# A two-layer graph network on one core: the order of the random walks, the projections' stationary, and how layer 1's targets reach the partitions

## The chip, the cores and the metric

The kernel runs on one core of a Trainium2 chip, in float32. The metric is the device time of one execution in microseconds (us). Engines are named as the profile names them: PE (TensorE matmul) with PEld (its weight load), DVE (VectorE), ACT (ScalarE), POOL (GpSimd), SP (SyncE, which here only issues DMAs).

## The reference

x has N = 2708 nodes of D = 256 features, adj is N x N. Two layers, each with a residual and a layer norm:

```
# layer 0
R = (adj + I) / rowsum
for n in (0, 1):
    A  = top_p(softmax((Xa W1^T W2^T)(Xa W3^T)^T), 0.9), rows renormalized
    Xf = R Xf;  Xa = A Xa                 # both start from x
    Z += Xf U1[n]^T + Xa U2[n]^T
x = layernorm(x + (layernorm(x + Z) * g + b))
# layer 1, 4 heads of 64
Wh = x W;  s_i = Wh a_src;  s_j = Wh a_dst
att = softmax_j(leaky_relu(s_i + s_j, 0.2) where adj != 0 or i == j)
x = layernorm(x + att Wh)
```

The part with R (the "walks") is R x U1[0]^T + R R x U1[1]^T. The part with A is the "attention".

## The kernel before, in words

The nodes are cut into NT = 22 row tiles (16 of 128 rows, 6 of 110). A block of the transposed adjacency is the stationary of a walk matmul, and 22 of them give one tile of a walk; there are two walks, so 2 x 22 x 22 = 968 walk matmuls (`walks()`, L845). The blocks come from memory by half tiles on SP's queue (`load`, through `by_tile`, L94), three buffers deep (`adjp`). A walk accumulates in the one PSUM bank of pool `ps_wk`.

**Layer 0, start.** `load_x` brings x into `xe` (its last column is 1, so the first walk also gives the row sums). Six groups of tiles are turned (PE transposes, L1045) and projected (L1056): a stationary `wq` = W1^T W2^T written twice side by side gives q on both halves of the partitions, and a second stationary `wk_sb` (W3^T twice) gives k on both. Both halves are needed because `scores` (L620) works on the two halves of the columns at once, with k of columns 0 to 1353 on partitions 0 to 63 and of the others on 64 to 127.

**The order written by hand.** After this, PE, ACT, DVE and POOL follow an order made by Python generators. SP and everything outside that block are ordered by the framework's planner. `slot(spend, begin)` advances the running searches (`going`) by one piece, may start the search of a later tile, advances the open epilogues (`doing`), and then emits `spend` walk matmuls (it stops at the end of a tile's walk; what is left of the spend is kept for the next slot). There are 10 slots in the fill, then in `step(0)` 22 tiles of 6 slots, a stretch between the steps, `step(1)` again with 22 tiles of 6 slots, and a tail. The spends are:

```python
SPEND_FIRST, SPEND_0 = 5, (2, 2, 2, 2, 2, 1)
SPEND_BETWEEN, SPEND_1 = 6, (5, 5, 4, 5, 5, 4)
```

In `step`, `weigh` transposes the attention weights `e` of the tile by groups (L202), ACT copies them (`eT`, L208) one group ahead, and PE multiplies (L217). A search is: scores on PE, exponentials on ACT (L624), in step 1 four passes of ACT over the row (L645), then candidates and sorting on DVE (L710 to L797). It starts three tiles ahead.

**Epilogues.** `after_walk0(t)`: DVE adds the tile's own row to the walk result (L858), PE turns it (`turn`, L603), and `terms1` (L890) multiplies it by both U1 matrices: one part goes, scaled and summed, to `c1` in memory, the other becomes `yw`, the input of walk 1. `after_attention0(t)`: turns the attention result, projects a pair of tiles for step 1 (`project`, L591), and `terms2` (L910) multiplies by both U2 matrices. `finish(t)`: ACT scales walk 1's result (L924), POOL adds `c1`, `c2` and the attention result held in `held`, then two layer norms, and `sources` computes layer 1's values and scores.

**Layer 1.** Targets are taken in three spans of 8, 8 and 6 tiles. `targets` puts exp(0.8 s_i) of a span on all partitions: for each tile and head a transpose with a broadcast stationary (L174) and an exponential on ACT (L179). Span 0's are made by `first_targets` during the last tile of step 1. Then for each of 22 source tiles: load the mask block (L1164), ACT makes it 0/1 (L1165, L1170), DVE forms four heads of weights (L1225), PE multiplies them (L1233, L1240). `settle` finishes a span.

Of the kernel before, what the change touches and what calls it, by code (L numbers as in the profile page):

```python
# [16 lines left out]
P = 128  # L17
# [19 lines left out]
SPEND_FIRST, SPEND_0 = 5, (2, 2, 2, 2, 2, 1)  # L37
SPEND_BETWEEN, SPEND_1 = 6, (5, 5, 4, 5, 5, 4)
HELD = 8
# [6 lines left out]
def kernel(  # L46
# [71 lines left out]
    def load_x():  # L118
        step = 4
        for t0 in range(0, NT, step):  # L120
            by_tile(xe[:, t0:, 0:D], x, t0, min(t0 + step, NT))
# [45 lines left out]
    def targets(g, r, aux):  # L167

        i0 = off[spans[g][0]]
        for t in spans[g]:  # L170
            m = rows[t]
            tr = aux()
            for h in range(H):
                nc.tensor.transpose(  # L174
                    tr[:, h, :m], s_src[:m, t, h : h + 1].to_broadcast([m, P]),
                    ident[:m, :m],
                )
            for k in range(2):
                nc.scalar.activation(  # L179
                    r[k][:, :, off[t] - i0 : off[t + 1] - i0], tr[:, 2 * k : 2 * k + 2, :m],  # L180
                    AF.Exp, scale=1.0 - NEG_SLOPE,
                )
            yield
# [41 lines left out]
    def general_layer0():  # L225
        with ExitStack() as l0:
# [8 lines left out]
            load_x()  # L235
# [248 lines left out]
    def fast_layer0(ep, adjp):  # L484
# [22 lines left out]
        wq = w0.tile([P, DC, 2, DA], F32, name="wq")  # L507
        wk_sb = w0.tile([P, DC, 2, DA], F32, name="wk_sb")
# [4 lines left out]
        w2_sb = tmp[:DA, P : 2 * P].rearrange("p (h e) -> p h e", h=2)  # L513
        w1_sb = heldp.tile([P, D], F32, name="xa1")[:DA].rearrange("p (c d) -> p c d", c=DC)
        nc.scalar.dma_start(w1_raw, w1T.rearrange("(c p) e -> p c e", p=P))
        for h in range(2):
            nc.scalar.dma_start(w2_sb[:, h, :], w2T)
        for h in range(2):
            nc.scalar.dma_start(wk_sb[:, :, h, :], w3T.rearrange("(c p) e -> p c e", p=P))
        load_x()  # L520
# [33 lines left out]
        yw = keep.tile([P, NT, D], F32, name="yw")  # L554
# [6 lines left out]
        c2 = [dram.tile([P, D], F32, name=f"c2_{t}") for t in range(NT)]  # L561

# [8 lines left out]
        for c in range(DC):  # L571
            tr = ps_tr.tile([P, 4, P], F32, name="tr")
            nc.tensor.matmul(
                tr[:, 0, :], w1_sb[:, c, :], w2_sb.rearrange("p h e -> p (h e)"),
                start=True, stop=True,
            )
            nc.vector.tensor_copy(wq[:, c].rearrange("p h e -> p (h e)"), tr[:, 0, :])

        def keep_k(s, c0, m, src, copy):
            low = max(0, min(HN - c0, m))  # L580
            if low:
                copy(kT[s][0:DA, c0 : c0 + low], src[0:DA, :low])
            if low < m:
                copy(kT[s][DA:P, c0 + low - HN : c0 + m - HN], src[DA:P, low:m])

        def project(s, c0, w, xT, copy_q, copy_k):

            pj = ps_tr.tile([P, 4, P], F32, name="tr").rearrange("p (n a) b -> p n (a b)", n=2)
            for n, wm in enumerate((wq, wk_sb)):
                for c in range(DC):  # L590
                    nc.tensor.matmul(  # L591
                        pj[:, n, :w], wm[:, c].rearrange("p h e -> p (h e)"), xT[:, c, :w],
                        start=(c == 0), stop=(c == DC - 1),
                    )
            copy_q(qT[:, c0 : c0 + w], pj[:, 0, :w])
            keep_k(s, c0, w, pj[:, 1], copy_k)
# [216 lines left out]
        def walks():  # L813
# [16 lines left out]
            for n, (s, t, j0, j1) in enumerate(queue):  # L830
                m = rows[t]
                cur, w = (xe, D + 1) if s == 0 else (yw, D)
# [5 lines left out]
                if j0 == 0:  # L838
                    ac = ps_wk.tile([P, CHUNK], F32, name="walk")
                    if s:  # L840
                        ca, cb = (finp.tile([P, D], F32, name=k) for k in ("ca", "cb"))
                        nc.sync.dma_start(ca[:m], c1[t][:m])
                        nc.sync.dma_start(cb[:m], c2[t][:m])
                for j in range(j0, j1):
# [4 lines left out]
                    if j == NT - 1:  # L849
                        doing.append(after_walk0(t, ac) if s == 0 else finish(t, ac, ca, cb))  # L850
# [3 lines left out]
        def after_walk0(t, ac):  # L854
            m = rows[t]
            unfinished.add(t)
            xf = rowp.tile([P, D + 1], F32, name="xf")
            nc.vector.tensor_add(xf[:m], ac[:m, : D + 1], xe[:m, t, :])  # L858
            nc.vector.reciprocal(rinv[:m, t : t + 1], xf[:m, D : D + 1])
            yield  # L860
            tp = ps_tr.tile([P, 4, P], F32, name="tr")
            xT = turn(xf, m, tp, nc.scalar.copy)
            yield
            terms1(t, xT)
# [4 lines left out]
        def after_attention0(t, xa):  # L869
# [10 lines left out]
            if t % 2:  # L880
                project(1, off[t - 1], 2 * m, both, nc.scalar.copy, nc.scalar.copy)
# [3 lines left out]
        def terms1(t, xT):  # L885
# [3 lines left out]
            for c in range(DC):  # L889
                nc.tensor.matmul(  # L890
                    cy[:m], xT[:, c, :m], u_sb[:, 0, c].rearrange("p s e -> p (s e)"),
                    start=(c == 0), stop=(c == DC - 1),
                )
            r = rinv[:m, t : t + 1]
            cs = rowp.tile([P, D], F32, name="cs")
            nc.scalar.activation(cs[:m], cy[:m, 0:D], AF.Copy, scale=r)
            nc.scalar.activation(yw[:m, t, :], cy[:m, D : 2 * D], AF.Copy, scale=r)

            own = rowp.tile([P, D], F32, name="own", bufs=1)
            nc.gpsimd.tensor_scalar(own[:m], yw[:m, t, :], r, None, op0=ALU.mult)  # L900
            nc.gpsimd.tensor_add(cs[:m], cs[:m], own[:m])
# [410 lines left out]
```

## Time and profile before

| | us |
|---|---|
| median of 3 runs | 1678.13 (1677.03 to 1678.82) |
| the profiled execution, its time | 1677.58 |
| the profiled execution, its span | 1675.8 |
| granted PE clock, mean | 0.992 |
| PE busy | 1610.0 |
| DVE busy | 1217.0 |
| ACT busy | 766.8 |
| POOL busy | 423.4 |
| first scores on PE (L620) | at 40.3 |
| first attention matmul of step 0 (L217) | at 71.7 |
| first attention matmul of step 1 | at 655.0 |
| last attention result of step 1 (L1005) | at 1280.0 |
| first matmul of layer 1 (L1233) | at 1298.1 |

The span runs from the first to the last instruction; the time also has what lies around it. "Busy" is the time in which an engine had an instruction running; a busy PE is not PE at its peak. A float32 matmul shows as two records in the profile, a transpose as one. In a table by stage each column gives an engine's busy us in that stretch and, in brackets, its instructions; behind them stand the granted PE clock, the share of the DMA engines' time, and GB/s.

### The profile page before, as it was taken

The page shows a single profiled execution, that of the slowest core. Times are in us where ns is not written, and L with a number is a line of the kernel's source. Part 1 is how long each engine was busy: PE and PEld are TensorE (multiplying, and loading weights), DVE is VectorE, ACT ScalarE, POOL GpSimd, SP SyncE. Part 2 cuts the span into 40 slices and gives each one's busy share as a digit, 9 for nine tenths or more (in the row PEclk, how much of TensorE's full clock was granted, in tenths as well). Part 3 has the DMA queues.
Part 4 walks back from the last instruction along what each step waited for, and adds up shares of the span by engine and source line. Part 5 has one row for each costly group of instructions (what it writes and reads, how often), then busy time and mean ns, then how long its engine had stood idle before and what let it go on. Part 6 is the DMA issues. An engine that isn't in the chain of part 4 may idle for free.

```text
span 1675.8 us, 23985 instructions
## 1 busy us (share of the span) xinstructions
PE 1610.0 (96%) x8218; PEld 1058.0 (63%) x8218; DVE 1217.0 (73%) x3660; ACT 766.8 (46%) x1324; POOL 423.4 (25%) x893
## 2 busy tenths in 40 slices
PE   7999999999999999999999999999997999999895
PEld 4677777777777776777787878777785222322332
DVE  2954554565455019888999999998994899888886
ACT  1333333333333255656576666667555334243231
POOL 0310111111011023223244444444434020420313
PEclk9999999999999999999999999999999999999998
DMA  6211011111110142212322322323222332232231
GB/s 166 73 47 46 26 43 40 40 31 40 40 43 25 43 104 67 63 49 73 79 72 79 87 68 82 89 58 77 72 65 88 98 99 86 88 93 77 76 86 39
DMA packets 153873, 113.89 MB, mean 68 GB/s; under 512 B 39898, under 2 KB 144094, under 8 KB 153742
## 3 DMA queue, kind: packets, MB, share of 16 engines
q1 hardware_dynamic: 149278, 105.18, 23.4%
q0 software_dynamic: 2112, 5.55, 1.0%
q10 hardware_dynamic: 2352, 1.54, 0.3%
q8 instruction: 67, 1.10, 0.3%
q14 instruction: 64, 0.52, 0.1%
HBM read 101.16 MB, written 11.09 MB: 67 GB/s over the span
## 4 chain that ended last, share of the span: by engine, by line
PE 78%; DVE 9%; ACT 5%; POOL 4%; issue 3%; DMA 0%; ACTq 0%; POOLq 0%; DVEq 0%; SPq 0%
PE att L217 23%; PE walk L845 19%; PE acc L1233 12%; PE acc L1240 6%; PE lg L620 5%; PE tr L202 4%; ACT e L624 3%; PE tr L910 2%; PE tr L890 2%; PE lg L1056 1%; PE tr L591 1%; DVE cand L725 1%; ACT eT L208 1%; DVE scr L791 1%; POOL res L1192 1%
## 5 line engine op out<-in xcount | busy, mean ns | idle before, releaser
L645 ACT ACTIVATE junk<-e,minus,rth 128x2708 bf16<-128x2708 f32 (+1 forms) x88 | 232.8, 2646 | 35.7 <-POOL rth L677 34.6
L845 PE MATMUL walk<-xe,blk 128*128 128x257 f32 (+3 forms) x968 | 240.5, 382 | 0.0
L217 PE MATMUL att<-ba,eT 128*128 128x256 f32 (+3 forms) x968 | 234.1, 383 | 5.0 <-ACT eT L208 5.0
L217 PE MATMUL att<-xe,eT 128*128 128x256 f32 (+3 forms) x968 | 233.3, 381 | 4.3 <-ACT eT L208 4.3
L208 ACT COPY eT<-tr 128x512 f32<-128x512 f32 (+5 forms) x264 | 138.2, 537 | 206.3 <-PE tr L202 206.1
L1233 PE MATMUL acc<-pt,v 128*64 128x512 f32 (+3 forms) x1056 | 226.0, 550 | 4.7 <-DVE pt L1225 3.8
L845 PE MATMUL walk<-yw,blk 128*128 128x256 f32 (+3 forms) x968 | 228.1, 381 | 1.7 <-ACT xw L924 1.7
L725 DVE MAX8 cand<-e 128x8 f32<-128x170 f32 (+1 forms) x352 | 89.2, 322 | 178.8 <-ACT e L624 178.8
L845 PEld LDWEIGHTS walk<-xe,blk 128*128 128x128 f32 (+3 forms) x968 | 174.6, 186 | 54.2 <-issue 29.3
L845 PEld LDWEIGHTS walk<-yw,blk 128*128 128x128 f32 (+3 forms) x968 | 176.7, 186 | 41.5 <-issue 11.5
L1225 DVE SCALAR_TENSOR_TENSOR pt<-e,tj,blk 128x1024 f32<-128x1024 f32 (+3 forms) x176 | 185.8, 1115 | 19.8 <-issue 8.0
L217 PEld LDWEIGHTS att<-ba,eT 128*128 128x128 f32 (+3 forms) x968 | 171.4, 186 | 32.7 <-ACT eT L208 10.0
L217 PEld LDWEIGHTS att<-xe,eT 128*128 128x128 f32 (+3 forms) x968 | 170.9, 186 | 30.9 <-ACT eT L208 7.2
L624 ACT ACTIVATE e<-lg 128x1024 f32<-128x1024 f32 (+1 forms) x132 | 121.1, 921 | 132.3 <-PE lg L620 132.3
L1233 PEld LDWEIGHTS acc<-pt,v 128*64 128x64 f32 (+1 forms) x1056 | 72.1, 137 | 153.5 <-issue 112.3
L202 PE MATMUL tr<-ident,e 128*128 128x128 f32 (+3 forms) x968 | 140.8, 270 | 4.6 <-ACT xT L606 3.8
L202 PEld LDWEIGHTS tr<-ident,e 128*128 128x128 f32 (+3 forms) x968 | 115.1, 139 | 32.3 <-ACT xT L606 6.1
L1165 ACT ACTIVATE blk<-blk 128x1024 f32<-128x1024 f32 (+3 forms) x66 | 63.2, 958 | 155.3 <-DMA blk<-in_adjT_dram 136.3
L1240 PE MATMUL acc<-pt,sb 128*32 128x512 f32 (+3 forms) x1056 | 124.5, 549 | 0.0
L1225 DVE SCALAR_TENSOR_TENSOR pt<-r,tj,blk 128x1024 f32<-128x1024 f32 (+1 forms) x88 | 109.8, 1306 | 10.8 <-issue 7.0
L631 POOL TENSOR_TENSOR fact<-zp 128x1 f32<-128x1 f32 (+1 forms) x44 | 24.8, 563 | 359.0 <-ACT e L624 349.1
L725 DVE MAX8 cand<-scr 128x8 f32<-128x97 f32 (+1 forms) x616 | 101.9, 243 | 0.0
(203 smaller groups left out, 1999.6 us busy)
## 6 DMA issues: line engine op xcount, KB each, us to landing
blk<-in_adjT_dram SPq DMA_DIRECT2D x32, 704.0 KB
blk<-in_adjT_dram SPq DMA_DIRECT2D x32, 512.0 KB
blk<-in_adjT_dram SPq DMA_DIRECT2D x48, 330.0 KB
blk<-in_adjT_dram SPq DMA_DIRECT2D x32, 320.0 KB
blk<-in_adjT_dram SPq DMA_DIRECT2D x12, 605.0 KB
blk<-in_adjT_dram SPq DMA_DIRECT2D x12, 440.0 KB
blk<-in_adjT_dram SPq DMA_DIRECT2D x18, 283.6 KB
c<-cs POOLq DMA_DIRECT2D x32, 128.0 KB, 2.1
```

Source lines behind the costliest of these rows:

```text
L202: nc.tensor.transpose(tr[: rows[t], q, :m], e[:m, off[t] : off[t + 1]], ident[:m, :m])
L208: copy(eT[:k, : len(grp), :m], tr[:k, : len(grp), :m])
L217: nc.tensor.matmul(acc, eT[: rows[t], q, :m], value(t), start=(t == 0), stop=(t == NT - 1),)
L620: nc.tensor.matmul(lg[:m, h, :w], qT[part, cols], kT[s][part, c0 : c0 + w], start=True, stop=True,)
L624: nc.scalar.activation(halves[:m, :, c0 : c0 + w], lg[:m, :, :w], AF.Exp, accum_out=zp[:m, n : n + 1],)
L645: nc.scalar.activation(junk[:m], e[:m], func, scale=rth, bias=minus1[:m], accum_out=acc)
L725: nc.vector.max(cand[:, n, :], src[:m, n * size : min(N, (n + 1) * size)])
L845: nc.tensor.matmul(ac[:m, :w], blk[: rows[j], j - j0, :m], cur[: rows[j], j, 0:w], start=(j == 0), stop=(j == NT - 1),)
L1165: nc.scalar.activation(bar, bar, AF.Sign)
L1225: nc.vector.scalar_tensor_tensor(pt[:k, :gw], r[h // 2][:k, h % 2, :gw], tj[:k, j, h : h + 1], mask, op0=ALU.max, op1=ALU.mult,)
L1233: nc.tensor.matmul(acc[h // 2][c][q * FO : (q + 1) * FO, :w], v[j][:k, h - 1 + q, :], pts[h - 1 + q][:k, c0 : c0 + w], **at,)
L1240: nc.tensor.matmul(acc[2][c][h * 32 : (h + 1) * 32, :w], sb[:k, j, h : h + 1].to_broadcast([k, 32]), pts[h][:k, c0 : c0 + w], **at,)
```

## The change

It has five parts.

1. **Walks factored.** The walk part is computed as R (x U1[0]^T + R (x U1[1]^T)). `terms1` no longer follows walk 0: it works on the turned x that the projections have made anyway (kept in `x_turned`, in the space of `ba`), writes x U1[0]^T to `c1` and x U1[1]^T into `xe`. x itself now lies in `xm`, which attention step 0 reads. Walk 0 runs on `xe`; its epilogue divides by the row sum, adds `c1` and overwrites x in `xm`, on DVE and POOL alone. Walk 1 runs on `xm`. `finish` loads x again from memory.
2. **The order.** No walk matmul is emitted in the fill or in step 0; the ten slots of the fill emit `terms1` instead. The spends of the other stretches rise. `finish` has fewer empty slots.
3. **One stationary for q and k.** k and q columns stand side by side in one stationary (`wkqk`), so one matmul pair gives k on the half where it is wanted and q on the other half; a DMA on POOL's queue copies q to the half where k is. A range that crosses column 1354 is cut there.
4. **Attention results of step 1** for tiles 0 to 17 go to memory (`c3`, on POOL's queue) and come back when the tile's second walk begins (on SP's queue).
5. **Targets through memory.** `share` makes one transpose and one exponential for a whole span (32 rows: tile and head) and stores it; `spread` reads it back with four DMAs of SP, each onto all 128 partitions.

```diff
-SPEND_FIRST, SPEND_0 = 5, (2, 2, 2, 2, 2, 1)
-SPEND_BETWEEN, SPEND_1 = 6, (5, 5, 4, 5, 5, 4)
-HELD = 8
+SPEND_BETWEEN, SPEND_1 = 7, (7, 6, 7, 7, 6, 7)
+HELD, WAITING = 6, 4
...
+    def share(g, tr):
+        span, m = spans[g], rows[spans[g][0]]
+        k = len(span) * H
+        nc.tensor.transpose(
+            tr[:k, 0, :m],
+            s_src[:m, span[0] : span[-1] + 1, :].rearrange("p t h -> p (t h)"), ident[:m, :m],
+        )
+        nc.scalar.activation(line[:k, :m], tr[:k, 0, :m], AF.Exp, scale=1.0 - NEG_SLOPE)
+        nc.sync.dma_start(shared[g], line[:k, :m])
+
+    def spread(g, r):
+        lines = shared[g].rearrange("(t h) m -> h t m", h=H)
+        n = len(spans[g]) * rows[spans[g][0]]
+        for k in range(2):
+            for h in range(2):
+                nc.sync.dma_start(
+                    r[k][:, h, :n].rearrange("p (t m) -> p t m", t=len(spans[g])),
+                    lines[2 * k + h].partition_broadcast(P),
+                )
...
+        def project(s, c0, w, pj, xT, copy_q, copy_k):
+            for lo, hi, h in ((c0, min(c0 + w, HN), 0), (max(c0, HN), c0 + w, 1)):
...
                 for c in range(DC):
                     nc.tensor.matmul(
-                        pj[:, n, :w], wm[:, c].rearrange("p h e -> p (h e)"), xT[:, c, :w],
-                        start=(c == 0), stop=(c == DC - 1),
+                        pj[:, at], wkqk[:, c, h : h + 2].rearrange("p h e -> p (h e)"),
+                        xT[:, c, at], start=(c == 0), stop=(c == DC - 1),
                     )
-            copy_q(qT[:, c0 : c0 + w], pj[:, 0, :w])
-            keep_k(s, c0, w, pj[:, 1], copy_k)
+                copy_k(kT[s][here, lo - h * HN : hi - h * HN], pj[here, at])
+                copy_q(qT[there, lo:hi], pj[there, at])
+                nc.gpsimd.dma_start(qT[here, lo:hi], qT[there, lo:hi])
...
-                cur, w = (xe, D + 1) if s == 0 else (yw, D)
+                cur, w = (xe, D + 1) if s == 0 else (xm, D)
...
+                    ca = finp.tile([P, D], F32, name="ca", bufs=4)
                     if s:
-                        ca, cb = (finp.tile([P, D], F32, name=k) for k in ("ca", "cb"))
+                        cb = finp.tile([P, D], F32, name="cb")
+                        nc.sync.dma_start(ca[:m], x[off[t] : off[t + 1], :])
+                        nc.sync.dma_start(cb[:m], c2[t][:m])
+                        if t in c3:
+                            held[t] = finp.tile([P, D], F32, name="cc")
+                            nc.sync.dma_start(held[t][:m], c3[t][:m])
+                    else:
                         nc.sync.dma_start(ca[:m], c1[t][:m])
-                        nc.sync.dma_start(cb[:m], c2[t][:m])
...
         def after_walk0(t, ac, ca):
...
             nc.vector.tensor_add(xf[:m], ac[:m, : D + 1], xe[:m, t, :])
-            nc.vector.reciprocal(rinv[:m, t : t + 1], xf[:m, D : D + 1])
+            nc.vector.reciprocal(r, xf[:m, D : D + 1])
             yield
-            tp = ps_tr.tile([P, 4, P], F32, name="tr")
-            xT = turn(xf, m, tp, nc.scalar.copy)
-            yield
-            terms1(t, xT)
+            nc.gpsimd.tensor_scalar(xf[:m, :D], xf[:m, :D], r, None, op0=ALU.mult)
+            nc.gpsimd.tensor_add(xm[:m, t, :], xf[:m, :D], ca[:m])
...
         def terms1(t, xT):
...
-            nc.scalar.activation(cs[:m], cy[:m, 0:D], AF.Copy, scale=r)
-            nc.scalar.activation(yw[:m, t, :], cy[:m, D : 2 * D], AF.Copy, scale=r)
-
-            own = rowp.tile([P, D], F32, name="own", bufs=1)
-            nc.gpsimd.tensor_scalar(own[:m], yw[:m, t, :], r, None, op0=ALU.mult)
-            nc.gpsimd.tensor_add(cs[:m], cs[:m], own[:m])
-            nc.gpsimd.tensor_add(cs[:m], cs[:m], xe[:m, t, 0:D])
+            nc.scalar.copy(cs[:m], cy[:m, 0:D])
+            nc.scalar.copy(xe[:m, t, 0:D], cy[:m, D : 2 * D])
             nc.gpsimd.dma_start(c1[t][:m], cs[:m])
...
         def finish(t, ac, ca, cb):
-            nc.scalar.activation(xw, ac[:m, :D], AF.Copy, scale=rinv[:m, t : t + 1])
+            nc.vector.tensor_add(xw, ac[:m, :D], xm[:m, t, :])
             yield
+            nc.scalar.activation(xw, xw, AF.Copy, scale=rinv[:m, t : t + 1])
...
         def step(s, cur, spend):
+                if s and t == NT - 2:
+                    share(0, ps_tr.tile([P, 4, P], F32, name="tr"))
                 if s and t == NT - 1:
-                    doing.append(first_targets())
+                    ahead.extend(room(ep))
+                    spread(0, ahead)
...
-                        if s:
+                        if s and t in c3:
+                            nc.gpsimd.dma_start(c3[t][:m], xa[:m])
+                            stored.add(t)
+                        elif s:
                             held[t] = xa
...
             for n in range(10):
-                slot(SPEND_FIRST if n else 0, (0, n // 4) if n in (0, 4, 9) else None)
+                slot(0, (0, n // 4) if n in (0, 4, 9) else None)
+                for t in range(n * NT // 10, (n + 1) * NT // 10):
+                    terms1(t, x_turned[:, :, off[t] : off[t + 1]])
             layer1_weights()
-            step(0, xe, SPEND_0)
+            step(0, xm, [0] * len(groups))
...
-                    list(targets(g + 1, r_next, aux))
+                    share(g + 1, aux())
+                    spread(g + 1, r_next)
```

## The prediction

> **What bounds the kernel now.** I read the page first, then a table of busy time by stage, then the chain of waits inside one step-0 tile, then the time line of the first 30 us.
>
> The page says that TensorE (PE) is full nearly everywhere:
>
> ```profile
> span 1675.8 us, 23985 instructions
> ...
> PE 1610.0 (96%) x8218; PEld 1058.0 (63%) x8218; DVE 1217.0 (73%) x3660; ACT 766.8 (46%) x1324; POOL 423.4 (25%) x893
> ...
> PE   7999999999999999999999999999997999999895
> ...
> DVE  2954554565455019888999999998994899888886
> ```
>
> Only 66 us of the span are without PE work. DVE is half idle in slices 5 to 17 and nearly full in slices 18 to 29. The stage table (busy us of PE, PEld, DVE, ACT, POOL) puts that in numbers: fill of the pipeline, attention step 0, the stretch between, step 1, the gap before layer 1, layer 1.
>
> ```profile
> 43.00:71.00 28.00, 27.48 (x123) 19.55 (x120) 25.92 (x94) 7.56 (x17) 10.26 (x13) 1.00 0.32 82
> 71.00:588.00 517.00, 509.18 (x2440) 376.51 (x2439) 261.27 (x958) 172.00 (x387) 56.41 (x124) 1.00 0.14 39
> 588.00:654.00 66.00, 62.70 (x269) 43.99 (x268) 28.27 (x109) 36.26 (x51) 21.01 (x49) 1.00 0.38 98
> 654.00:1280.00 626.00, 614.95 (x3026) 482.42 (x3024) 562.15 (x2094) 402.00 (x659) 244.52 (x550) 1.00 0.27 70
> 1280.00:1298.00 18.00, 11.26 (x63) 8.00 (x60) 11.18 (x16) 10.68 (x46) 11.25 (x14) 0.91 0.55 166
> ```
>
> So moving walk matmuls from step 0 to step 1 moves PE time, it does not remove it. What counts is PE work deleted, and waits that appear or go where the walks served as filler. The chain through a step-0 tile shows the one place where filler already covers a wait:
>
> ```profile
> 235.80 1.08 PE lg L620 x4
> ...
> 236.91 2.12 ACT e L624 x4
> 239.03 0.48 ACT eT L208
> ...
> 239.56 2.00 PE att L217 x8
> ...
> 242.68 0.87 PE walk L845 x4
> ```
>
> At the head of a tile the first attention matmul waits for two exponentials and a copy on ACT, 3.76 us after the scores begin, whatever PE does meanwhile. Behind it the chain is PE alone. A "walk x4" piece is two matmuls (two records each): 0.435 us a walk matmul.
>
> **The change part by part.** Unit prices from that chain and its neighbours: walk matmul 0.435, `terms1` or `terms2` 1.72, `turn` about 0.4 with its wait, `project` of a tile pair 1.73, targets of one tile 0.44 (four transposes, as "tr x4").
>
> How many walk matmuls each stage holds I counted by stepping the hand-written order: slots times spend. Before: 44 in the fill, 243 in step 0, 96 between, 585 in step 1. After: 0, 0, 110, 858. Both sum to 968.
>
> *First projections.* The time line:
>
> ```profile
> 10.73 3.78 PE L1056 MATMUL lg<-e,wq 128*128 128x512 f32 x4 [0.99 <-ACT e L1051]
> ...
> 18.28 1.99 PE L1056 MATMUL lg<-e,wq 128*128 128x512 f32 x4 [0.67 <-ACT e L1051]
> 20.10 1.88 PE L1056 MATMUL lg<-e,wk_sb 128*128 128x512 f32 x4
> ```
>
> A group repeats every 5.3 us; one stationary for q and k deletes the second matmul pair: 1.7 us for each of three warm full groups, 1.46 and 0.73 for the short ones, about 2.4 for the first: 9.7 us. The copies (0.6 on ACT, 0.7 on DVE per group) fit in the 3.5 us that remain. The first row runs at half the later speed. [...] By the row, speed came at about 15 us after some 4.5 us without a break; the changed order still has 3.4 us of slow matmuls and 1.3 of transposes in a row. I take +1, and keep 0 to +10.7.
>
> The second copy of q goes through a POOL-issued SBUF transfer, whose cost for this path is not in the trace; nearest row: `c<-cs`, 2.1 us to landing, issue about 0.6. The first scores read columns copied four groups earlier, so 0 if they wait only for these, +3 if for the last copy. I take +1. Sum of the part: -7.7, scores start near 32.5 instead of 40.3.
>
> *Fill.* Out: 44 walks (19.1), one `turn` and `terms1` (2.1). In: all 22 `terms1`, 37.8 us. Net +16.6. Each has 0.75 us of ACT copies and a 0.65 us DMA issue on POOL, under 1.72 of PE; `cs` has two buffers, so its round trip (copy, issue, 2.1 landing: about 3.4) just fits two `terms1`. If it didn't, 0.3 us each, +6: upper end.
>
> *Step 0.* A tile pair lasts 48.4 us in the chain. Out: 20 of its 22 walks (8.7), the two at the heads being worth nothing because ACT's 3.76 us stands; a `turn` (0.4), a `terms1` (1.8), half a `project` (0.86). That is 11.8 a pair, 36.6 left; 11 pairs give -129. DVE falls from 11.9 us a tile to about 11.6 against 18.3, so it does not become the bound; searches start three tiles ahead. The q transfer sits behind ACT's copy in POOL's queue, where only small sums of the search wait (POOL is 11% busy). Lower cover elsewhere: ACT's copies of `eT` have 1.73 us of attention matmuls above them, enough for 0.59.
>
> *Between.* +14 walks (+6.1), less four `terms1` (6.9), four `turn` (1.5), half a `project` (0.9): -3.2. The adjacency blocks are there, since SP loads them long before.
>
> *Step 1.* +273 walks (+118.8), less six `terms1`, five `turn` and six tiles of targets (14.8). PE then has about 709 us. The tile grows from 28.5 to about 33 us while DVE has about 26 to 28 us of work (562 us before, plus 17 sums of walk 0 at 0.6 and 22 sums of walk 1 at 0.43: 582 over some 725, 80% instead of 90%). So some of the 11 us without PE work and of the DVE pieces in the chain go: I take -8, bounds -15 and 0. Against it, every walk result now leaves the only walk bank by DVE, not by ACT, behind DVE's search work. 39 such ends fall here; I take 0.15 us each, +6, bounds 0 and +25. SP has 22 more loads, 18 reloads of stored attention results (stored at least half a tile earlier; POOL issues these stores) and waits for buffers in between; a half block of walks is 9.6 us and loads are two half blocks ahead, so 2 to 5 us of SP waiting stay covered; without that cover they would fall on PE once per walk. Net +102.
>
> *Gap and layer 1.* The gap of 18 us is one tile's chain through POOL and DVE after the last attention; the removed slots hold nothing to wait for: -1. Targets of spans 1 and 2 on PE: span 1 sits in the gap (0.5 counts), span 2 costs 6 x 0.44: -3.1. The spread puts 2 MB per span (1.35 for the last) on SP's queue ahead of the mask blocks, behind the landing of the small store. Nearest rows: loads of x ran at 322 to 350 GB/s in 3 to 12 us, so 6 us of transfer, 2.1 for the store's landing, 1.4 for issues: about 10 against three block buffers of 5.44 us an iteration. I take +2, bounds -2 and +15.
>
> Sum: -7.7 + 16.6 - 129 - 3.2 + 102 - 4.1 + 2 = -23.4. The profiled execution took 1677.6 us (span 1675.8), so 1654.2; the median of the runs is 0.5 higher than that execution.
>
> **The rivals.**
> *More gain (0.18).* DVE's relief in step 1 is whole and nothing new waits: -38, 1640. For it: DVE pieces carry the chain at 850 and 1178 to 1256 us. Against: PE shows only 11 us idle in step 1.
> *The spread lands on layer 1 (0.15).* SP stands at the small store, the mask blocks come late twice: up to +15, with a slower start +5: 1672. For: the masks already arrive just before use. Against: the gap has DMA engines at 0.55 only, and the targets of span 1 were done there already.
> *Slower: the one walk bank (0.09).* In step 1, PE's next walk waits until DVE has read the bank. A pass of DVE is 3.05 us; from 23.4/39 = 0.6 us per walk end the whole gain is gone, at 1.2 us the time is 1677. With 1.5 each, 1690. For: DVE was 90% busy. Against: a slot of att and transposes (2.2 us) lies between, and DVE gets 5 us more per tile.
> *It does not do what it says (0.04).* The second copy of q and the reloads could cost what the halved projections give, about 20 us in all: 1677, no difference.
>
> **How the numbers follow.** Main case 0.54, with its own range 1643 to 1664. 0.2% is 3.4 us, about what a measurement of this kernel can tell from none. Faster: main, more gain, and nearly all of the spread case: 0.86. Same: 0.05. Slower: 0.09. Predicted 1654; the range runs from the more-gain case's near side to the spread case, 1637 to 1672.
>
> **What would show it.** Right: first scores near 32 us, attention of step 0 starting near 77 and tiles of about 18.3 us, its end near 470 with no walk row before; projection groups with half the matmuls; step-1 tiles of about 33 us with DVE near 80%; first layer-1 matmul near 1275, then 377 us. Wrong: step-0 tiles above 19.5 (a new wait at ACT or a PSUM bank), walk rows idle behind the DVE sums by over 20 us, layer 1 over 385 with masks waiting on DMA, or slow projection matmuls up to the scores.

## The result and the profile after

The changed kernel takes 1657.25 us (median of 4 runs, 1656.57 to 1657.84), the kernel before in the same session 1678.08: a ratio of 0.9876, 95% interval 0.9859 to 0.9893. That is 20.8 us less; 24 were predicted. The profiled span fell by 20.5 us, from 1675.8 to 1655.3.

The page of the changed kernel, the same lines as were shown of before:

```profile
span 1655.3 us, 23835 instructions
...
PE 1577.3 (95%) x8029; PEld 1035.8 (63%) x8029; DVE 1229.6 (74%) x3682; ACT 742.3 (45%) x1263; POOL 430.1 (26%) x908
...
PE   7999999999999999999999999999997999999894
...
DVE  3676667666508877876888888987873999899795
```

PE lost 32.7 us of work, but the span only 20.5: time without PE work rose from 65.8 to 78.0 us. DVE's full stretch in the middle is looser: in slices 18 to 29 its digits are 6 to 9, mostly 8, where before has 8 and mostly 9.

The table by stage of the changed kernel (stretch, its length, busy us of PE, PEld, DVE, ACT and POOL with instruction counts in brackets, granted clock, DMA share, GB/s): fill, step 0, the stretch between, step 1, the gap, layer 1 with the end.

```profile
43.00:78.00 35.00, 35.00 (x93) 14.30 (x91) 24.37 (x83) 16.43 (x46) 9.93 (x20) 1.00 0.22 72
78.00:468.00 390.00, 371.70 (x1851) 269.48 (x1850) 249.76 (x920) 155.17 (x356) 31.66 (x95) 1.00 0.03 10
468.00:530.00 62.00, 59.61 (x264) 45.39 (x263) 28.46 (x110) 32.78 (x40) 15.65 (x43) 1.00 0.42 112
530.00:1254.00 724.00, 717.67 (x3516) 576.37 (x3515) 582.25 (x2142) 392.65 (x624) 273.93 (x582) 1.00 0.36 95
1254.00:1274.00 20.00, 8.60 (x24) 4.45 (x22) 12.27 (x18) 8.05 (x35) 10.13 (x11) 0.55 0.62 185
```

Read it against the table of before. Step 0 is 390 us long instead of 517 and has lost its filler: 18.3 us without PE work where there were 7.8. Step 1 is 724 instead of 626, and its idle time fell from 11.1 to 6.3. The last row is the surprise: PE works 8.6 us in the gap instead of 11.3, and the granted clock, as a mean over the stretch, is 0.55 instead of 0.91.

From one mark in the trace to the next (first scores, first and last attention matmul of a step, last attention result, first layer 1 matmul, end), the stages moved so:

| stage | predicted | measured |
|---|---|---|
| to the first scores | -7.7 | 40.27 to 31.49: -8.8 |
| fill | +16.6 | +16.0 |
| step 0 | -129 | -126.7 |
| between | -3.2 | -4.1 |
| step 1 | +102 | +98.1 |
| gap | -1 | +1.7 |
| layer 1 and end | -3.1 + 2 | +3.4 |
| sum | -23.4 | -20.5 |

At the end of attention the changed kernel is 25.6 us ahead (1280.04 to 1254.45), 4.3 more than predicted; behind it 5.1 are given back.

### The profile page after: what moved, and what is told of

It is laid out like the page before. It is cut to its first block, busy times and chain, and to the rows that moved or that the text cites. A ratio compares the mean times of both kernels' runs of the same rounds, so it can differ in the third digit from the quotient of the medians.

```text
span 1655.3 us, 23835 instructions
## 1 busy us (share of the span) xinstructions
PE 1577.3 (95%) x8029; PEld 1035.8 (63%) x8029; DVE 1229.6 (74%) x3682; ACT 742.3 (45%) x1263; POOL 430.1 (26%) x908
## 5 line engine op out<-in xcount | busy, mean ns | idle before, releaser
L227 PE MATMUL att<-xm,eT 128*128 128x256 f32 (+3 forms) x968 | 229.3, 381 | 17.4 <-ACT eT L218 17.4
L656 ACT ACTIVATE junk<-e,minus,rth 128x2708 bf16<-128x2708 f32 (+1 forms) x88 | 232.8, 2646 | 14.6 <-POOL rth L688 13.7
L863 PE MATMUL walk<-xe,blk 128*128 128x257 f32 (+3 forms) x968 | 223.8, 382 | 1.9 <-DVE xf L877 1.8
L863 PE MATMUL walk<-xm,blk 128*128 128x256 f32 (+3 forms) x968 | 221.8, 380 | 0.0
L863 PEld LDWEIGHTS walk<-xe,blk 128*128 128x128 f32 (+3 forms) x968 | 177.3, 185 | 46.7 <-issue 13.7
L227 PEld LDWEIGHTS att<-xm,eT 128*128 128x128 f32 (+3 forms) x968 | 171.2, 186 | 44.7 <-ACT eT L218 22.2
L863 PEld LDWEIGHTS walk<-xm,blk 128*128 128x128 f32 (+3 forms) x968 | 177.8, 186 | 32.9 <-issue 4.9
L227 PEld LDWEIGHTS att<-ba,eT 128*128 128x128 f32 (+3 forms) x968 | 171.0, 186 | 32.6 <-ACT eT L218 10.2
L877 DVE TENSOR_TENSOR xf<-walk,xe 128x257 f32<-128x257 f32 (+1 forms) x22 | 9.4, 426 | 112.4 <-PE walk L863 112.4
```

The costliest lines, as they stand in the source:

```text
L227: nc.tensor.matmul(acc, eT[: rows[t], q, :m], value(t), start=(t == 0), stop=(t == NT - 1),)
L656: nc.scalar.activation(junk[:m], e[:m], func, scale=rth, bias=minus1[:m], accum_out=acc)
L863: nc.tensor.matmul(ac[:m, :w], blk[: rows[j], j - j0, :m], cur[: rows[j], j, 0:w], start=(j == 0), stop=(j == NT - 1),)
```

## The experiments

The theory at the start: the change works through deleted and regrouped PE work, and what is missing was lost in and behind the gap. The rival: the loss comes from layer 1's targets going through memory, late mask blocks above all.

**One part alone: one stationary for q and k.** The kernel before, with the second projection and its stationary taken out:

```diff
-            for n, wm in enumerate((wq, wk_sb)):
-                for c in range(DC):
-                    nc.tensor.matmul(pj[:, n, :w], wm[:, c]...)
+                for c in range(DC):
+                    nc.tensor.matmul(pj[:, at], wkqk[:, c, h : h + 2]..., xT[:, c, at], ...)
+                copy_k(kT[s][here, ...], pj[here, at])
+                copy_q(qT[there, lo:hi], pj[there, at])
+                nc.gpsimd.dma_start(qT[here, lo:hi], qT[there, lo:hi])
```

> The kernel before with one part of the change alone: q and k from one stationary, q copied to the other half by a transfer. Theory (PE is full, so the matmul time deleted is the gain): the first scores come 8.8 us earlier, as in the changed kernel, and 11 tile pairs of step 0 lose half a projection, 0.86 each, 9.5 us; together 18 us, 1660, most of the 20.5 us of the whole change. Rival (the walks' new form carries the gain): this part alone gives 10 or less, 1668 or more, and step-0 tile pairs stay at 48.4 us because something else sets them.

Measured: 1660.08 us (1659.49 to 1661.07), ratio 0.9891 (0.9876 to 0.9906): -17.8 against the 1677.85 of before in these runs. The prediction's terms for this part alone are -7.7 (first projections), 11 times -0.86 (step 0's pairs) and -0.9: -18.1. The trace has 8.3 us by the first attention matmul and 15.7 by the end of step 0. So most of what the whole change gains is this one edit. What the other parts add shows in the marks of the two kernels: the last attention matmul of step 1 starts at 1263.0 with this edit alone and at 1252.6 in the changed kernel, 10.4 us earlier, but the end comes only 2.8 us earlier (1660.08 to 1657.25). The next runs ask where the 7.6 went. A part of it is lost ahead of the gap: ACT takes the result of the last attention tile 1.85 us after that last matmul's start in the changed kernel (1254.45) and 0.41 us after it with this edit alone, because two passes over a mask block (from 1252.31 and 1253.50) stand ahead of it on ACT.

**One part alone: targets through memory.** The kernel before with `share` and `spread` in place of its transposes, for all three spans:

```diff
-                if s and t == NT - 1:
-                    doing.append(first_targets())
+                if s and t == NT - 2:
+                    share(0, ps_tr.tile([P, 4, P], F32, name="tr"))
+                if s and t == NT - 1:
+                    ahead.extend(room(ep))
+                    spread(0, ahead)
...
-                    list(targets(g + 1, r_next, aux))
+                    share(g + 1, aux())
+                    spread(g + 1, r_next)
```

> The kernel before with another part alone: layer 1's targets through memory. Theory (without the targets' transposes PE idles in the gap before layer 1 and drops to half clock): 3.5 us of PE work at the end of step 1 and 2.6 in span 2 go, but the gap's last projections take 2.1 instead of 1.05 us and the first 16 accumulating matmuls of layer 1 take 6.5 instead of 3.65, about 5 us lost; within 2 us of 1678 either way. Rival (the transposes were plain cost): 6 us faster, 1672. Second rival (the spread delays the mask blocks): idle PE behind them in layer 1, 1682 or more.

Measured: 1679.06 us, ratio 1.0005 (0.9997 to 1.0013): no difference, although 3 transposes stand in place of 88. The time line of PE in the gap and at the start of layer 1, first in the kernel before, then in this one (start, us, engine, line, operation; in brackets the idle time ahead and what ended it):

```profile
1288.40 0.46 PE L142 MATMUL tr<-ident,xe 110*128 110x110 f32 x2 [3.89 <-DVE xe L944]
1289.29 2.10 PE L148 MATMUL tr<-wx,xT 128*110 128x264 f32 x4 [0.22 <-ACT xT L144]
...
1295.72 1.14 PE L148 MATMUL tr<-wx,xT 128*110 128x264 f32 x4
...
1298.14 3.65 PE L1233 MATMUL acc<-pt,v 128*64 128x512 f32 x16 [0.83 <-issue]
```

```profile
1287.88 0.60 PE L142 MATMUL tr<-ident,xe 110*128 110x110 f32 x2 [7.90 <-DVE xe L955]
...
1298.94 6.38 PE L1240 MATMUL acc<-pt,v 128*64 128x512 f32 x16 [1.36 <-ACT cs L158]
```

The first group takes 6.38 us instead of 3.65. In the kernel before, PE's longest wait in the gap is 3.89 us, and behind it PE is slow too: a projection takes 2.10 us, and the granted clock is 0.50 from 1288.6 to 1292.0 us. But transposes of span 1's targets follow, the next projection takes 1.14 us again, and the first layer 1 matmuls are at full speed. With the transposes taken out of the gap, the clock falls to 0.50 at 1284.0 us, inside a wait of 7.90 us, and is back only at 1304.5 us, near the end of the first group.

The changed kernel has the same. Its PE rows around the gap, with SP's read-back of span 1's targets and ACT's next mask block:

```profile
1253.65 1.14 PE L147 MATMUL tr<-wx,xT 128*110 128x264 f32 x4 [0.67 <-ACT xT L143]
...
1256.25 2.10 PE L147 MATMUL tr<-wx,xT 128*110 128x264 f32 x4 [1.15 <-ACT xT L143]
1263.27 0.60 PE L141 MATMUL tr<-ident,xe 110*128 110x110 f32 x2 [4.92 <-DVE xe L955]
1264.30 2.10 PE L147 MATMUL tr<-wx,xT 128*110 128x264 f32 x4 [0.43 <-ACT xT L143]
1269.93 0.60 PE L141 MATMUL tr<-ident,xe 110*128 110x110 f32 x2 [3.53 <-DVE xe L955]
1270.96 2.10 PE L147 MATMUL tr<-wx,xT 128*110 128x264 f32 x4 [0.43 <-ACT xT L143]
1274.29 6.50 PE L1241 MATMUL acc<-pt,v 128*64 128x512 f32 x16 [1.23 <-ACT cs L157]
...
1276.25 6.46 SPq L190 DMA_DIRECT2D r<-shared  x4
...
1291.20 1.06 ACT L1171 ACTIVATE blk<-blk 128x1024 f32<-128x1024 f32 x1 [14.22 <-DMA blk<-in_adjT_dram]
```

Projections take 2.10 us instead of the 1.05 to 1.14 of warm ones, the first group 6.50 instead of 3.65. The granted clock is 0.50 from 1256.2 to 1280.0 us and 1.00 on both sides. In the kernel with the targets alone it fell inside the wait of 7.90 us. Here it fell not in the waits of 4.92 and 3.53 us but ahead of both, just before the projection at 1256.25, where no wait had been longer than 1.15 us. In the 4.00 us from 1252.20 to 1256.20 PE was busy for 2.23 us.

ACT's wait of 14.22 us for its mask block is not the work of the read-back: SP issues that load at 1287.62, when DVE has just left the buffer (1287.59), and in the next kernel, which has no read-back there, ACT waits 11.18 us at the same place.

**Warm the gap: unread transposes.** The changed kernel with 96 transposes that nobody reads, each four on a tile of their own, placed ahead of layer 1's loops:

```diff
+        else:
+            for _ in range(24):
+                tr = aux()
+                for h in range(H):
+                    nc.tensor.transpose(tr[:, h, :], s_src[:, 0, h : h + 1].to_broadcast([P, P]), ident)
```

> The changed kernel with 96 added transposes whose results nothing reads, most of them placed in the gap before layer 1; transfers as before. Theory (half clock in the gap is the loss): the first 16 accumulating matmuls take 3.65 instead of 6.5 us and the last projections 1.05 instead of 2.1; 3 to 5 us faster than the changed kernel, 1653, although PE does more work. Rival (the clock there costs nothing that is waited for, or it is the transfers): same or slower by up to 2 us.

Measured: 1656.87 us, ratio 0.9872 (0.9857 to 0.9887): next to nothing. The first group did become warm (1274.48, 3.65 us), and the second began at 1279.92 instead of 1282.57, the 2.65 us that were looked for. At 1391.3 only 1.0 of them was left. The time lines of SP, ACT and DVE in this kernel show where:

```profile
1337.93 5.61 SPq L190 DMA_DIRECT2D r<-shared  x4
1350.84 1.06 ACT L1171 ACTIVATE blk<-blk 128x1024 f32<-128x1024 f32 x1 [9.42 <-DMA blk<-in_adjT_dram]
1354.08 11.86 DVE L1240 SCALAR_TENSOR_TENSOR pt<-e,tj,blk 128x1024 f32<-128x1024 f32 x9 [3.68 <-ACT blk L1176]
```

The 24 tiles passed through the two PSUM buffers that `share(1)` uses too, and the read-back of span 1's targets moved from 1276 to 1338 us. There it stands directly ahead of a mask block (issued at 1343.65, when the read-back ends) that still has to pass ACT, POOL and ACT: DVE waited 3.68 us and PE lost 1.65. So the rival has its truth as well: the four read-backs do hold up the masks behind them, and what they cost depends on where they stand.

**Span 1's targets by transposes again.** The other way to fill the gap:

```diff
-                    share(g + 1, aux())
-                    spread(g + 1, r_next)
+                    if g:
+                        share(g + 1, aux())
+                        spread(g + 1, r_next)
+                    else:
+                        list(targets(g + 1, r_next, aux))
```

> The changed kernel with the targets of span 1 alone made by transposes again, as before the change; spans 0 and 2 through memory. Theory (clock): the 32 transposes keep PE at full clock through the gap: first accumulating matmuls 3.65 us, 3 to 5 us faster than the changed kernel, 1653. Rival (the transposes in the gap hold up the last tiles, as they did before): no faster than 1657.

Measured: 1661.33 us, ratio 0.9898 (0.9882 to 0.9913), 4.1 us slower than the changed kernel. It is no clean test of the clock: only 4 of the 32 transposes fell in the gap, the first group was cold still (5.48 us), and 24 stand inside layer 1, from 1336.5 to 1341.9 us. It prices them there: 3.4 us of PE, and a last layer 1 matmul 4.2 us later than in the changed kernel. Why they moved there was not followed up.

**Warm the gap and leave the read-back where it was.** All 80 transposes on one PSUM tile:

```diff
+        else:
+            tr = aux()
+            for _ in range(20):
+                for h in range(H):
+                    nc.tensor.transpose(tr[:, h, :], s_src[:, 0, h : h + 1].to_broadcast([P, P]), ident)
```

> Edit: the changed kernel with 80 transposes on PE, written to one PSUM tile that nobody reads, in the 20 us gap between the last attention tile and layer 1; unlike the earlier kernel with 96 of them in 24 tiles, the read-back of span 1's targets stays at its place ahead of the mask blocks (that kernel had moved it from 1276 to 1338 us, where one mask block came 3.7 us late for DVE and PE lost 1.6 us). Theory 'the cold start costs 2.7 us and the earlier kernel lost it again only through the late mask block': first group of layer 1 matmuls 3.65 us instead of 6.50, the second at about 1280, and the end 2 to 3 us earlier, 1654 to 1655.5. Rival 'the slow start only covered the read-back': with the read-back at its old place the mask blocks behind it (ACT waits 14.2 us for one in the changed kernel) come late for a PE that is 2.7 us ahead, a wait of PE for DVE pt appears before 1300 us, and the time stays at 1656.5 to 1657.5.

Measured: 1654.23 us (1653.64 to 1654.65), ratio 0.9859 (0.9844 to 0.9874): 3.0 us faster than the changed kernel, and the span 3.8 us shorter. PE's time line:

```profile
1273.28 3.65 PE L1248 MATMUL acc<-pt,v 128*64 128x512 f32 x16 [0.57 <-ACT cs L157]
...
1278.72 3.65 PE L1248 MATMUL acc<-pt,v 128*64 128x512 f32 x16
```

The clock still falls in the gap (0.50 around 1264 to 1266 us), but the transposes bring it back: the last projection takes 1.05 us, so layer 1 starts 1.0 us earlier, its second group begins at 1278.72 instead of 1282.57, and this time the 3.85 us last to the end (last DVE operation at 1641.3 instead of 1645.1). The read-back is at 1276 again and PE's period of 5.44 us stands behind it. The slow start was a loss, not a cover for the read-back.

**The end of the program.** From the start of the last DVE operation to the end of the span it is 7.45 us in the kernel before (1668.35 to 1675.8), 6.7 with one stationary alone, and 10.2 in the changed one (1645.10 to 1655.3). In all three the span ends 0.8 us after the longest DRAIN of POOL. POOL's DRAIN rows (number, then shortest, median and longest ns, then the starts of the first and the last), in the order before, one stationary, changed:

```profile
L1308 POOLq DRAIN  x3: 40/107/3663, 1671.3 to 1675.5; - x3
```

```profile
L1300 POOLq DRAIN  x3: 40/107/5215, 1652.4 to 1658.2; - x3
```

```profile
L1316 POOLq DRAIN  x3: 40/107/6685, 1647.8 to 1655.0; - x3
```

The change adds DMAs that POOL issues: 19 q copies and 18 stored attention results, to 44 of before. 44, 63 and 81 DMAs, 3663, 5215 and 6685 ns: a mean of 83 ns for each, although in the changed kernel most of them landed a millisecond earlier and the last was issued at 1129.0 us. Issued from SP instead:

```diff
-                nc.gpsimd.dma_start(qT[here, lo:hi], qT[there, lo:hi])
+                nc.sync.dma_start(qT[here, lo:hi], qT[there, lo:hi])
...
-            nc.gpsimd.dma_start(c1[t][:m], cs[:m])
+            nc.sync.dma_start(c1[t][:m], cs[:m])
```

and likewise in `terms2` and for `c3`.

> Edit: the changed kernel with all four DMA issues that stand on POOL (the q copies and the rows put away by terms1, terms2 and xa) issued from SP instead; everything else as changed. Question: in the changed kernel the last DVE operation starts at 1645.10 and the span ends at 1655.3, 10.2 us later, against 7.45 us in the kernel before (1668.35 to 1675.8); in both the end waits for a DRAIN of POOL, of 6.69 us there and 3.66 before, 5.22 with one stationary for q and k alone. Theory 'the drain grows with the DMAs that POOL has issued in the whole program' (software queue packets 2112, 2784 and 3648 in these three kernels for 3.66, 5.22 and 6.69 us): with none left the drain is under 1 us, the end follows the last DVE operation by some 4 to 6 us, and the time is 1651 to 1654, 3 to 6 us under the changed kernel's 1657.25. Rival 1, the drain belongs to the program's length or to the last stores: it stays at 6.7 us, time 1657. Rival 2, SP's queue is in order and each put-away waits for an ACT copy, so the pattern loads behind it come late and the walks' matmuls wait: 1660 or more, seen as PE waiting for DMA blk or ca in the two steps.

Measured: 1653.08 us (1652.05 to 1653.49), ratio 0.9849 (0.9834 to 0.9864): 4.2 us faster than the changed kernel. Its row:

```profile
L1316 POOLq DRAIN  x3: 34/50/82, 1648.0 to 1651.1; - x3
```

The drain is gone, the end follows 6.3 us behind the last DVE operation, and no mark ahead of it moved by more than 0.15 us (step 1's attention starts at 531.5 against 531.4). The stores on SP's queue delayed nothing that can be seen.

Both fixes together:

> Edit: both together, all POOL DMAs on SP and the 80 unread transposes in the gap. If both theories hold the gains add, as one is at the start of layer 1 and the other behind the last store: 1648 to 1652. If only one holds: that one's time. If SP's in-order queue holds loads back: above 1657.

Measured: 1649.49 us (1648.80 to 1650.07), ratio 0.9829 (0.9815 to 0.9842). The two gains, 3.0 and 4.2, sum to 7.2; together they give 7.8.

Does the drain cost the kernels without the whole change anything?

> Edit: the kernel before with its two DMA issues on POOL issued from SP; nothing else. Its end is 7.45 us behind the last DVE operation, with a POOL DRAIN of 3.66 us; the changed kernel's was 10.2 us with a drain of 6.69 us, and 6.1 us with no drain left. Theory 'the drain is on the path for what it exceeds of about 2.5 us': the drain falls to below 0.2 us and the time by 1.2 us, to 1676 to 1677. Rival 'in the kernel before the drain was hidden': 1677.8 as before.

> Edit: the kernel before with one stationary for q and k, and all POOL DMAs on SP. It had 1660.08 us with them on POOL and ended 6.7 us behind its last DVE operation, its drain of 5.22 us having begun 2.2 us earlier than in the others. Theory 'the drain cost it less than 1 us': 1659 to 1660, so that with the tail equal on both sides the factored walks, the new order and the targets together are worth 1659.5 - 1653.1 = 6 us, not the 3 us that 1660.08 - 1657.25 shows. Rival 'the drain costs its whole length': 1655.

Measured: 1678.48 us (ratio 1.0003, 0.9995 to 1.0011) and 1659.60 us (0.9890, 0.9874 to 0.9905): no difference for either. In the first the end did come closer, 6.1 us behind the last DVE operation instead of 7.45, but step 1's attention starts at 656.9 instead of 655.0 us. SP's queue is the cause that comes to mind, since SP is held 17.5 us there by `terms2`'s stores, which wait for ACT's copy. The trace speaks against it: after the weights at the very start PE waits for no DMA in either kernel. What differs is PE's clock. The same walk piece, in the kernel before and then in this one:

```profile
649.59 0.41 PE L603 MATMUL tr<-ident,xf 110*128 110x110 f32 x2 [1.79 <-DVE xf L858]
649.83 4.08 PE L845 MATMUL walk<-xe,blk 128*110 128x257 f32 x18
```

```profile
649.80 0.41 PE L603 MATMUL tr<-ident,xf 110*128 110x110 f32 x2 [2.50 <-DVE xf L858]
650.05 5.76 PE L845 MATMUL walk<-xe,blk 128*110 128x257 f32 x18
```

PE stood ready 0.5 us earlier and DVE, busy with the search, was done 0.2 us later. So PE waited 2.50 us instead of 1.79, the granted clock was 0.50 from 650.3 to 653.7 us, and the piece took 1.7 us longer, more than the 1.35 us won at the end. The first theory was right on the drain and wrong on the time, and its rival, that the drain was hidden, is not shown by the equal times. With the second kernel, the rest of the change can be priced with equal ends: 1659.60 to 1653.08 is 6.5 us, not the 2.8 that the plain comparison gives, and with the gap warmed as well (1649.49) 10.1, close to the 10.4 seen at the last attention matmul.

**The heads of step 0.** The prediction let ACT's wait at the head of each tile stand. In the changed kernel its row says that 17.4 us of PE's time go there (busy us, mean ns, then the idle time ahead and what ended it), and next to it stand the two walks:

```profile
L227 PE MATMUL att<-xm,eT 128*128 128x256 f32 (+3 forms) x968 | 229.3, 381 | 17.4 <-ACT eT L218 17.4
...
L863 PE MATMUL walk<-xe,blk 128*128 128x257 f32 (+3 forms) x968 | 223.8, 382 | 1.9 <-DVE xf L877 1.8
L863 PE MATMUL walk<-xm,blk 128*128 128x256 f32 (+3 forms) x968 | 221.8, 380 | 0.0
```

The fill ahead, meanwhile, is PE alone: 35.00 of 35.00 us. So six tiles of `terms1` were moved from the fill into the heads of step 0's tiles 0 to 11, one matmul of the pair in each:

```diff
+                if s == 0 and t < 2 * len(LATE):
+                    n = LATE[t // 2]
+                    if t % 2 == 0:
+                        late[:] = [ps_wk.tile([P, CHUNK], F32, name="walk")]
+                    terms1(n, x_turned[:, :, off[n] : off[n + 1]], (t % 2,), late[0])
...
-                for t in range(n * NT // 10, (n + 1) * NT // 10):
+                for t in EARLY[n * len(EARLY) // 10 : (n + 1) * len(EARLY) // 10]:
```

> Edit: the changed kernel with the c-rows matmuls of source tiles 15 to 20 (terms1, 6 pairs of 128x512 at 0.86 us each matmul) taken out of the fill ahead of the first attention tile and put one matmul at a time into the heads of step 0's tiles 0 to 11, where PE waits about 0.8 us for ACT's exps (att waits for eT by 17.4 us over 22 tiles). Theory 'the fill is bound by PE, and the heads of step 0 are bound by ACT': the fill ends 10.3 us earlier (first attention matmul at 68 to 69 instead of 78.9), step 0 stays within 2 us of its 389 us, and the time is 1647 to 1649. Rival 'the fill's end is set by the exps on ACT or by q's way through the copies': the first attention matmul moves by less than 4 us and the time stays within 3 of 1657. Rival 'the heads are bound by PE too': the fill gets shorter but step 0 longer by the same 10 us, 1657 again.

Measured: 1651.49 us (1651.00 to 1651.94), ratio 0.9842 (0.9828 to 0.9855): 5.8 us faster than the changed kernel, where 8 to 10 were expected. The fill gives 9.1 us (first attention matmul at 69.8 instead of 78.9), and step 0 takes 3.5 of them back (392.6 instead of 389.1 us). The row says why:

```profile
L227 PE MATMUL att<-xm,eT 128*128 128x256 f32 (+3 forms) x968 | 229.3, 381 | 11.3 <-ACT eT L218 11.3
```

Only 6.1 us of wait went for 10.3 us of matmuls put in, though the wait is about 0.8 us a tile and one matmul 0.86. The idea holds; its size was taken too large, 5.8 us coming of 8 to 10.

**All three fixes.**

> Edit: the changed kernel with the three edits together: POOL's DMAs on SP, 80 unread transposes in the gap ahead of layer 1, and source tiles 15 to 20 of terms1 in the heads of step 0. The first two measured 1649.49 together and the third -5.8 us alone, in another stage; if the gains add, 1643 to 1645, and the last attention matmul of step 1 near 1247. If the put-aways of the rows, now on SP and in step 0, hold up the loads of step 1's first tiles: above 1647.

Measured: 1643.21 us (1642.91 to 1643.97), ratio 0.9794 (0.9781 to 0.9807), 34.9 us under the kernel before and 14.0 under the changed one. It is the fastest of all the kernels here. The three gains alone, 3.0, 4.2 and 5.8, sum to 13.0. In its trace the granted clock stays at 1.00 all through the gap (projections of 1.05 to 1.14 us), which it did in neither of the other two kernels with 80 transposes (one projection of 1.90 and one of 2.10 us).

## Why the prediction was right, and where it was not

The mechanism up to the last attention tile was right, stage by stage. That the total came within 3 us is in part luck: 4.3 us more than forecast were gained ahead of the gap, and 7.2 us fewer in it and behind it.

- *First projections* (-7.7, measured -8.8): right in mechanism. The upper end kept for the clock, +10.7, did not come; it was the author's estimate for later groups that stay as slow as the first, whose matmuls took 3.78 us in the kernel before where the second group's took 1.99. In the changed kernel's time line the first group is slow and the second is not:

```profile
10.04 3.78 PE L601 MATMUL lg<-ba,wkqk 128*128 128x512 f32 x4 [1.23 <-ACT ba L1062]
15.82 1.98 PE L601 MATMUL lg<-ba,wkqk 128*128 128x512 f32 x4 [1.12 <-ACT ba L1062]
```

  The slow matmuls and the transposes behind them filled PE without a break, as the prediction had counted, and the clock was up by the second group. The waits of 1.1 us did not bring it down: the granted clock stays at 1.00 from 13.7 to 1256.1 us, though PE was busy for only 2.88 of the 4.00 us from 13.60. Of the two allowances of +1, for the clock and for the q copy, about one was too much.
- *Fill* (+16.6, measured +16.0): 22 `terms1` at 1.72 us in a row, no wait for the two `cs` buffers.
- *Step 0* (-129, measured -126.7): as worked out, tiles of 17.7 us. That the head walks were worth nothing is confirmed by the waits for `eT`, which rose from 4.3 to 17.4 us over the 22 tiles.
- *Between* (-3.2, measured -4.1): no new wait.
- *Step 1* (+102, measured +98.1): DVE is at 582 of 724 us, 80%, as forecast. The terms mis-sized are the +6 for walk ends behind DVE, whose rows above show 1.9 us and 0.0, and the -8 for relief: PE's idle time fell by 4.8. The rival of the one walk bank had no ground. Two slips of the working cost nothing: PE's "about 709 us" is 719 by its own terms (717.7 measured), and the sums of the one-bank rival do not agree with each other (if 0.6 us per walk end takes the whole gain, 1.2 us gives 1701, not 1677). In the profile of before, DVE is half idle in slices 3 to 13 and nearly full from 16 on, not 5 to 17 and 18 on.
- *Gap and layer 1* (-4.1, and +2 for the spread; measured together +5.1): this is the step that failed. "The removed slots hold nothing to wait for" missed the point: the transposes in the gap brought PE's clock back before layer 1. Without them the first group of layer 1 costs 2.85 us more and the gap 1.7 instead of -1, of which 1.0 is the cold projection at its end. The clock was weighed at the front, where it did nothing, and not in the 20 us gap, where the change takes filler away. Inside layer 1, 2.2 us were won, 1.8 of them where span 2's transposes had stood; the forecast for these was 2.6.
- *The end* was in no term: nothing was put down for it, without a reason. The price of a POOL DMA was taken as its issue, 0.6 us under other work, and its landing. The 37 added ones came with 3.0 us more of drain (3.66 to 6.69), 82 ns each; the end came 2.75 us later.
- *Spread* (+2): not shown by itself. Its issues take SP 6.46 us, and PE keeps its period behind them. The same read-back 62 us later costs PE 1.65.

What stays open: the rest of the gap's +1.7 us, why the clock fell in it ahead of the long waits, and why the drain of the kernel with one stationary alone starts 0.6 us behind the last DVE operation and the others' 2.7 to 3.0 us. The order of the walks was not tried apart from their factoring, nor the stored attention results apart from both.

## What to carry to other kernels

Before you delete work that costs nothing, ask what it does besides: filler in a gap may keep PE's clock up or bring it back, and its loss shows in the stage behind the gap (here the first group of layer 1, 6.50 us without the transposes and 3.65 with them). When edits gain in one place, set marks along the trace (first and last instruction of each stage) and follow the gain to the end; here 7.6 of 10.4 us were lost again, most of it in the first group behind the gap and at the end of the program, which no row of the costliest groups names. And look at the granted clock before blaming a queue: in the kernel before with its stores on SP, it was the clock that took 1.7 us, not the queue. Last, count what an engine's DMAs leave behind: a queue that looks idle can still lengthen the end (here POOL's, with no DMA after 1129.0 us and a DRAIN of 6.69 us from 1647.8 us on).

## What the runs showed of the hardware that was not expected

- POOL's longest DRAIN at the program's end took 3.66, 5.22 and 6.69 us in the kernels where POOL had issued 44, 63 and 81 DMAs (before, one stationary, changed), a mean of 83 ns for each, and 0.08 us where SP issued them all. Taking it away brought the end of the span 3.9 us closer to the last DVE operation in the changed kernel (10.2 to 6.3), 1.35 us in the kernel before (7.45 to 6.1, lost again elsewhere).
- Four read-backs that spread 512 KB each over all partitions (from 4 KB each in memory) occupy SP's issue for 5.6 to 6.5 us when they stand in a row, where a mask block of 128x1024 takes 0.33 us. In the kernel with the targets alone, where other work stands between them, the first and the last take 0.39 and 0.36 us.
- PE's clock fell without a long idle stretch ahead of it. In the changed kernel it fell behind 4.00 us in which PE was busy for 2.23 us and waited 1.15 us at most at a time, and cost 2.85 us in the first sixteen-record group of layer 1 (6.50 instead of 3.65); with 80 transposes that nobody reads in the gap the group took 3.65 us again. The length of a wait does not tell by itself: one of 2.92 us ends at 1256.86 in the fastest kernel and one of 2.92 us at 1263.37 in the kernel with the first two fixes, and the next projection takes 1.14 us in the one and 2.10 in the other.
